# Grouped softmax, shared row memory and early loads in a two-layer graph attention kernel

## The chip, the cores and the metric

The kernel runs on one core of a Trainium2 chip. The core has TensorE (PE), VectorE (DVE), ScalarE (ACT), GpSimd (POOL) and SyncE (SP), and 16 DMA engines. The metric is the device time of one execution in microseconds; the figure shown for a kernel is the median of its runs.

## The reference

A graph of 10,000 nodes and 170,000 edges (80,000 random edges in both directions, and a loop at each node) goes through two graph attention layers, with residuals and layer norms. All of it is in float32; cut to what matters:

```python
def gat_conv(x, edge_index, W, a_src, a_dst, bias, heads, out_ch, concat):
    ...
    xl = (x @ W).reshape(n, heads, out_ch)
    alpha_src = jnp.einsum('nhc,hc->nh', xl, a_src)
    alpha_dst = jnp.einsum('nhc,hc->nh', xl, a_dst)
    e = jax.nn.leaky_relu(alpha_src[src] + alpha_dst[dst], 0.2)
    m = jax.ops.segment_max(e, dst, num_segments=n)
    e = jnp.exp(e - m[dst])
    s = jax.ops.segment_sum(e, dst, num_segments=n)
    alpha = e / (s[dst] + 1e-16)
    msg = xl[src] * alpha[:, :, None]
    out = jax.ops.segment_sum(msg, dst, num_segments=n)
    ...

h = gat_conv(x, edge_index, W1, a_src1, a_dst1, b1, 4, 256, True)
h = relu(layer_norm(h, g1, be1)) + (x @ Wr1 + br1)
h1 = h
h = gat_conv(h, edge_index, W2, a_src2, a_dst2, b2, 1, 768, False)
h = layer_norm(h, g2, be2) + (h1 @ Wr2 + br2)
return _layernorm(x + h)
```

`gat_conv` adds each node's loop a second time, so that a loop counts double (`doubled` in the kernel). Layer 1 has 4 heads of 256 columns (1024 in all), layer 2 one head of 768.

## The kernel before

**Stages.** First the kernel multiplies x by W1, node tile by node tile of 128 nodes (79 tiles), adds the two attention products of each node, and stores rows of 1033 numbers in a DRAM table (table1). Beside that it sorts the nodes by their number of edges and makes lists of neighbours. Then `ordered_layer1` and `ordered_layer2` each go through the 79 tiles. A tile holds 128 nodes with about equally many neighbours, and its work is done in "slots" or rows: row k holds, for each of the 128 nodes, the table row of its k-th neighbour. A tile has between 8 and 41 rows, 1377 in all. Layer 1's turns go up from 8 rows to 26, then take the tile of 41, then 27, 25, 24 and down to 9. Tiles of 22 rows and more are turns 34 to 45; turns 32, 33, 46 and 47 have 21 rows. Layer 2 goes from small to large tiles.

**The ring.** Rows are gathered from DRAM by GpSimd (L425, an indirect DMA for each row) into a ring of row places (`Ring`, 29 places of 1033 numbers in layer 1, 41 of 770 in layer 2). When row k of a tile is done with, `ring.fetch` asks for the row 29 (or 41) places further on. So a row's place must be free before its successor is asked for. After the logits of a set of rows, GpSimd also reads their last column (L490) and overwrites their attention columns (L491), in its own order between the gathers.

**A tile of layer 1.** `logits` (L479 to L487) adds the source and destination products of all of a tile's rows, applies the leaky relu, takes the maximum, subtracts it (VectorE) and takes the exponent (ScalarE). `normalised` (L498 to L504) divides by the sum. The weighted sum over the rows is then made by three engines. For the first `on_pe(t)` rows, at most 4, ScalarE makes diagonal matrices of the weights (L730) and TensorE multiplies them with the rows into a PSUM buffer acc (L736). Of the other rows VectorE does every fourth alone, with four multiply-adds of 256 columns (L521); for the rest ScalarE multiplies the row by its weights (L510) and VectorE adds it with one addition of 1024 columns (L517). ScalarE's multiplications are issued three rows ahead (`LEAD`). All of this is an order written out by hand, engine by engine (`manual_schedule`).

The generator `weights_of` does the logits and TensorE's share, and it is started for tile t+1 three rows before tile t ends, so that the next tile's logits stand in VectorE's order between the last rows of tile t. This is done only if the next tile's rows and 3 more fit in the ring (`SLOTS[t + 1] + LEAD <= ring.size`): not for the tiles of 27 and 41 rows. At the beginning of tile t come the layer norm of tile t-1 (`deviation`, `scaled`, L807), its transposition and the transposition of x (L708), the product with Wr1 (L172, 24 matmul records), and, two rows after TensorE's rows, `to_layer2` (L824 to L829): a store of the transposed h to h1_d and the product with W2 for layer 2's table, whose result is copied and stored by `store` in the next tile (L766, L768). `next_x` gathers the next tile's x and stores it to x_d (L697).

**The tile of 41 rows** doesn't fit the ring and goes through `attend_parts`: three parts, each with its own logits, a running maximum, sums on VectorE in a tile h of its own, and a rescaling of h when the maximum changes.

**Between the layers.** Layer 1's ring lies in a memory pool of that layer, layer 2's in one of its own, which may be used when layer 1's last store is through. Wr2 is loaded into Wr1's place by the first line of `ordered_layer2`. Then come, on SyncE's queue, h1 and x of the first two tiles (L911, L912) and five vectors spread over the partitions (L144), and on GpSimd's the gathers. br1 times Wr2 is made by TensorE: br1 is spread over 128 columns (brT, L905) and multiplied with Wr2 (`product`), then the residuals of tiles 0 and 1 (L988, L991), with tile 0's sums (L946) between them. The result of br1 times Wr2 is read after tile 0.

Of the kernel before, what the change touches and what calls it, by code (L numbers as in the profile page):

```python
# [35 lines left out]
P = 128  # L36
# [17 lines left out]
PARTED2 = 26  # L54

# [25 lines left out]
def gnn_kernel(ctx, tc, x, x_cols, src, dst, src_col, dst_col, W1, a_src1, a_dst1, b1, g1, be1, Wr1, br1,  # L81
# [359 lines left out]
    class Ring:  # L441
# [4 lines left out]
        def __init__(self, pool, table, row, size, own, at=None):  # L446
            self.table, self.size, self.own, self.issued = table, size, own, 0
            self.at = at or list(range(TOTAL))
            self.rows = pool.tile([P, size, row], F32, name="ring")
# [11 lines left out]

        def slot(self, q):
            return self.rows[:, q % self.size, :]

        def parts(self, lo, hi):

            while lo < hi:
                r = lo % self.size
                m = min(hi - lo, self.size - r)
                yield lo, lo + m, self.rows[:, r:r + m, :]  # L470
                lo += m
# [51 lines left out]

    def attend_parts(small, ring, acc, h_, ad, heads, dh, t, summed, between):


        c = heads * dh
        groups = -(-SLOTS[t] * 2 // ring.size)
        cuts = [FIRST[t] + SLOTS[t] * g // groups for g in range(groups + 1)]
        top = total = sums = None  # L530
        nc.vector.memset(acc[:, :c], 0.0)
        for lo, hi in zip(cuts, cuts[1:]):
            e, new = logits(small, ring, lo, hi, ad, heads, c, top)
            if lo == FIRST[t]:
                doubled(e, t)
            part = small.tile([P, heads], F32, name="part")
            nc.vector.reduce_sum(part, e.rearrange("p k h -> p h k"), axis=AX.X)
            if top is not None:
                nc.vector.tensor_add(acc[:, :c], acc[:, :c], sums[:, :c])
                fade = small.tile([P, heads], F32, name="fade")  # L540
                nc.vector.tensor_sub(fade, top, new)
                nc.scalar.activation(fade, fade, AF.Exp)
                for h in range(heads):
                    s = slice(h * dh, (h + 1) * dh)
                    nc.vector.tensor_scalar(acc[:, s], acc[:, s], fade[:, h:h + 1], None, op0=OP.mult)
                nc.vector.tensor_mul(fade, total, fade)
                nc.vector.tensor_add(part, part, fade)
            top, total = new, part
            m = min(ON_PE1, hi - lo - 1)
            pe = lo if hi == cuts[-1] else hi - m  # L550
            steps = summed(pe, e[:, pe - lo:], m)
            sums = next(steps)
            if pe == lo:
                for _ in steps:
                    pass
            alone = [q for q in range(lo, hi) if not pe <= q < pe + m]
            for k, q in enumerate(alone):
                shared = k >= len(alone) // 3
                if shared:
                    multiply(ring.slot(q), e[:, q - lo], dh)  # L560
                if k == len(alone) // 3 + 1:
                    for _ in steps:
                        pass
                weigh(acc, ring.slot(q), e[:, q - lo], dh, shared=shared)
                ring.fetch(q + 1 + ring.size)
            ring.fetch(hi + ring.size)
            between.pop(0)()
        nc.vector.tensor_add(acc[:, :c], acc[:, :c], sums[:, :c])
        divided(small, h_, acc, total, None, heads, dh)
# [111 lines left out]
    SLOTS1, FIRST1 = SLOTS, FIRST  # L681

# [3 lines left out]
    def ordered_layer1():  # L686
        nc.scalar.add_instruction(mybir.InstLoadActFuncSet(name=nc.get_next_instruction_name(), act_func_set_id=6, engine=nc.scalar.engine))
        with tc.tile_pool(name="b1", bufs=1) as pool, tc.tile_pool(name="small1", bufs=2) as small, \
                tc.tile_pool(name="ps_acc1", bufs=2, space=PSUM) as ps_acc, \
                tc.tile_pool(name="ps_h1", bufs=2, space=PSUM) as ps_half, \  # L690
                tc.tile_pool(name="ps_r1", bufs=1, space=PSUM) as ps_r, tc.manual_schedule():
            ring = Ring(pool, table1, R1, RING1, {})
# [25 lines left out]
            ring.fetch(RING1)  # L718
            g1_b, be1_b = (spread(pool, v, n) for v, n in ((g1, "g1"), (be1, "be1")))

            def on_pe(t):


                return min(max(SLOTS[t] // 2 - 5, 1), ON_PE1, SLOTS[t])

# [15 lines left out]
            def weights_of(t):  # L741

                n, m = SLOTS[t], on_pe(t)
                e, _ = logits(small, ring, FIRST[t], FIRST[t] + n, ring.slot(FIRST[t])[:, C1:C1 + H1], H1, C1)
                yield e
                normalised(small, e, H1, t)
                acc = ps_acc.tile([P, 2 * BANK], F32, name="acc")
                diagonals = pool.tile([P, ON_PE1 * H1, P], F32, name="diagonals")
                for lo, hi in ((0, min(m, 2)), (min(m, 2), m)):
                    summed(acc, diagonals, e, FIRST[t], lo, hi, m)  # L750
                    yield acc

            def shared(t, k):
                return (k - on_pe(t)) % SHARE > 0
# [16 lines left out]
            xT, moves = from_x(0)  # L771
            for move in moves:
                move()
            r = product(xT, wr1, C1, ps_r)
            for t in range(NT + 1):
# [3 lines left out]
                whole = live and n <= ring.size  # L779
                if whole and not ready:  # L780
                    ahead = weights_of(t)
                    ready += itertools.islice(ahead, 2)

                def multiplied(upto):
                    nonlocal done
                    while whole and done < min(upto, n):
                        if shared(t, done):
                            multiply(ring.slot(FIRST[t] + done), e[:, done], DH1)
                        done += 1

                if whole:
                    e, acc = ready
# [3 lines left out]
                for _ in ahead:  # L796
                    pass
# [6 lines left out]
                if last:  # L804
                    h = pool.tile([P, C1], F32, name="h")
                    scaled(h, [means[:, :C1]], stats, g1_b, be1_b)
                    nc.vector.scalar_tensor_tensor(h, h, 0.0, r_before[:, :C1], op0=OP.max, op1=OP.add)  # L807
                for move in moves:
                    move()
# [9 lines left out]
                if whole:  # L819
                    by_wr1()  # L820
# [12 lines left out]
                if last:  # L833
                    events.append((first + 2, to_layer2))
# [5 lines left out]
                if t + 1 < NT:  # L840
                    events.append((first + 2, next_x))

# [4 lines left out]
                if live and not whole:  # L847
                    due(first + 1)
                    sums, acc = (ps_acc.tile([P, 2 * BANK], F32, name="acc") for _ in range(2))
                    ad = small.tile([P, H1], F32, name="ad")  # L850
                    nc.vector.tensor_copy(ad, ring.slot(FIRST[t])[:, C1:C1 + H1])

                    def some(q, e, m):
                        diagonals = pool.tile([P, ON_PE1 * H1, P], F32, name="diagonals")
                        for lo, hi in ((0, min(m, 2)), (min(m, 2), m)):
                            summed(sums, diagonals, e, q, lo, hi, m)
                            yield sums

                    h = pool.tile([P, C1], F32, name="h")
                    attend_parts(small, ring, h, acc, ad, H1, DH1, t, some,  # L860
# [481 lines left out]
```

## Time and profile before

| what | us |
|---|---|
| median of the runs shown (3 runs) | 5579.29 |
| lowest and highest of these | 5576.32, 5603.79 |
| the profiled execution's own time | 5572.26 |
| its span, first to last instruction | 5570.4 |
| TensorE busy in the span | 4887.3 (88%) |
| VectorE busy | 4269.6 (77%) |
| GpSimd busy | 3301.6 (59%) |
| ScalarE busy | 2815.1 (51%) |
| bytes moved by DMA | 1591.39 MB |

All of the readings are of the one profiled execution. A busy engine is one whose instructions overlap the time; TensorE's matmuls are pipelined, so its busy share isn't a share of its peak. The granted clock is the share of full speed that the throttle gave TensorE. "Idle before" is the time in which an engine stood still before a group of instructions, with what ended it. Lines like L521 are lines of the kernel before; in the changed kernel the numbers are others. In lists of stretches, the first column is the stretch from and to, in us from the span's start.

### The profile page before, as it was taken

What the parts mean: (1) busy time and instruction counts of PE and PEld (TensorE: products, weight loads), DVE (VectorE), ACT (ScalarE), POOL (GpSimd) and SP (SyncE); (2) the same over time, 40 slices, a digit from 0 to 9 for tenths busy, and PEclk for the clock granted to TensorE, in tenths of its full rate; (3) what the DMA queues carried; (4) which work ended last, traced back from release to release, by engine and by line L of the source; (5) the groups of instructions that cost most, each with busy time, mean ns of one, the idle gap of its engine ahead of it and who ended that gap; (6) DMA issues with size and microseconds to landing.
All of it is one profiled execution on the core that took longest, in us unless ns stands there. A gap on an engine that the chain in (4) does not pass through costs nothing. (4 is left out here: it accounts for less than half of the span.)

```text
span 5570.4 us, 59760 instructions
## 1 busy us (share of the span) xinstructions
PE 4887.3 (88%) x15188; PEld 2896.9 (52%) x15191; DVE 4269.6 (77%) x7513; ACT 2815.1 (51%) x8193; POOL 3301.6 (59%) x3407
## 2 busy tenths in 40 slices
PE   9999996999999876689999999899988888887775
PEld 3444443555565544455555555565655555554544
DVE  5883344999999887789999995888876776766676
ACT  3443343777878776678877773333322222222222
POOL 2446455556666666566666653666665666666664
PEclk9999998999999987899999999999998888888887
DMA  4323536999999987899999986999888888888885
GB/s 156 123 94 89 91 97 234 323 345 354 364 366 371 350 325 255 314 342 369 370 367 361 339 310 230 334 336 329 323 322 287 307 298 301 295 291 294 293 293 183
DMA packets 474308, 1591.39 MB, mean 286 GB/s; under 512 B 118327, under 2 KB 122487, under 8 KB 473958
## 3 DMA queue, kind: packets, MB, share of 16 engines
q0 software_dynamic: 322384, 1286.62, 64.5%
q1 hardware_dynamic: 149520, 297.43, 15.8%
q10 hardware_dynamic: 2054, 3.42, 0.2%
q8 instruction: 128, 2.10, 0.1%
q14 instruction: 222, 1.82, 0.1%
HBM read 1431.80 MB, written 177.29 MB: 289 GB/s over the span
## 5 line engine op out<-in xcount | busy, mean ns | idle before, releaser
L425 POOL DMA_INDIRECT ring<-table,slots x2675 | 2664.3, 996 | 1631.5 <-issue 662.2
L521 DVE SCALAR_TENSOR_TENSOR acc<-ring,e,acc 128x512 f32<-128x512 f32 (+1 forms) x2530 | 1579.0, 624 | 149.4 <-PE acc L736 46.5
L510 ACT ACTIVATE ring<-ring,e 128x256 f32<-128x256 f32 x3284 | 1338.4, 508 | 2.3 <-issue 2.2
L517 DVE TENSOR_TENSOR acc<-acc,ring 128x1024 f32<-128x1024 f32 x801 | 986.5, 1232 | 70.5 <-DVE acc L517 1.4
L991 PE MATMUL big<-wr,w 128*128 128x512 f32 (+1 forms) x2464 | 872.0, 500 | 111.3 <-issue 109.8
L946 PE MATMUL big<-ring,diagonals 128*128 128x256 f32 x2754 | 758.5, 433 | 206.8 <-issue 168.0
L172 PE MATMUL big<-w,xT 128*128 128x512 f32 x1896 | 827.2, 598 | 23.3 <-DMA w<-in_W_dram 9.4
L172 PE MATMUL big<-wr,xT 128*128 128x512 f32 x1896 | 831.7, 595 | 0.2 <-issue 0.2
L829 PE MATMUL half<-w,hT 128*128 128x512 f32 (+1 forms) x2528 | 830.4, 486 | 0.0
L946 PEld LDWEIGHTS big<-ring,diagonals 128*128 128x128 f32 x2754 | 593.8, 219 | 371.5 <-issue 235.1
L991 PEld LDWEIGHTS big<-wr,w 128*128 128x128 f32 x2464 | 481.3, 196 | 471.4 <-issue 439.5
L945 ACT ACTIVATE diagonals<-ident,e 128x128 f32<-128x128 f32 x1377 | 423.5, 388 | 598.4 <-remote 180.3
L829 PEld LDWEIGHTS half<-w,hT 128*128 128x128 f32 x2528 | 477.8, 189 | 372.3 <-issue 334.4
L736 PE MATMUL acc<-ring,diagonals 128*128 128x256 f32 x1912 | 474.8, 406 | 201.9 <-ACT diagonals L730 198.0
L172 PEld LDWEIGHTS big<-w,xT 128*128 128x128 f32 x1896 | 362.7, 192 | 483.7 <-issue 464.9
L172 PEld LDWEIGHTS big<-wr,xT 128*128 128x128 f32 x1896 | 356.0, 191 | 419.4 <-issue 419.4
L736 PEld LDWEIGHTS acc<-ring,diagonals 128*128 128x128 f32 x1912 | 384.6, 204 | 285.0 <-ACT diagonals L730 219.0
L583 ACT ACTIVATE sd<-mv,eps 128x1 f32<-128x1 f32 x237 | 69.3, 293 | 696.9 <-DVE mv L581 444.4
L667 DVE TENSOR_TENSOR scr<-big,ad_b 128x1024 f32<-128x1024 f32 x79 | 96.7, 1224 | 378.4 <-ACT row L664 330.7
L730 ACT ACTIVATE diagonals<-ident,e 128x128 f32<-128x128 f32 x956 | 293.0, 388 | 173.3 <-DVE e L501 144.6
L672 POOL TENSOR_TENSOR row<-row,none 128x1024 f32<-128x1024 f32 x79 | 187.2, 2369 | 264.5 <-ACT row L664 261.5
L670 ACT ACTIVATE scr<-scr 128x256 f32<-128x256 f32 x632 | 253.5, 402 | 120.3 <-DVE scr L667 120.3
(185 smaller groups left out, 3445.0 us busy)
## 6 DMA issues: line engine op xcount, KB each, us to landing
ring<-table,slots POOLq DMA_INDIRECT x2675
table<-row SPq DMA_DIRECT2D x79, 516.0 KB
h_d<-hT SPq DMA_DIRECT2D x79, 512.0 KB
w<-h_d SPq DMA_DIRECT2D x77, 512.0 KB
table<-row SPq DMA_DIRECT2D x79, 385.0 KB
ring<-table SPq DMA_DIRECT2D x79, 385.0 KB
xT<-in_x_cols_dram SPq DMA_DIRECT2D x79, 384.0 KB
x_d<-xt SPq DMA_DIRECT2D x79, 384.0 KB
```

Source lines behind the costliest of these rows:

```text
L172: nc.tensor.matmul(p[:, c:e], aT[:, j, :], w[:, j, c:e], start=(j == 0), stop=(j == k - 1))
L425: nc.gpsimd.indirect_dma_start(out=to, out_offset=None, in_=table, in_offset=bass.IndirectOffsetOnAxis(ap=index, axis=0), **more)
L510: nc.scalar.activation(row[:, s], row[:, s], AF.Copy, scale=e[:, h:h + 1])
L517: nc.vector.tensor_add(acc[:, :c], acc[:, :c], row[:, :c])
L521: nc.vector.scalar_tensor_tensor(acc[:, s], row[:, s], e[:, h:h + 1], (acc if first is None else first)[:, s], op0=OP.mult, op1=OP.add)
L670: nc.scalar.activation(m[:, s], m[:, s], AF.Copy, accum_out=row[:, C1 + i * H1 + h:C1 + i * H1 + h + 1])
L730: nc.scalar.activation(diagonals[:, k * H1 + i, :], ident, AF.Copy, scale=e[:, k, i:i + 1])
L736: nc.tensor.matmul(acc[:, c:d], diagonals[:, k * H1 + i, :], ring.slot(q + k)[:, c:d], start=(k == 0 and c % BANK == 0), stop=(k == m - 1 ...
L829: nc.tensor.matmul(q, hT[:, j, :], w2[:, j, c:c + q.shape[1]], start=(j == 0), stop=(j == K1 - 1))
L945: nc.scalar.activation(diagonals[:, (k - lo) % G, :], ident, AF.Copy, scale=e[:, k - lo, :])
L946: nc.tensor.matmul(to, diagonals[:, (k - lo) % G, :], ring.slot(at + k)[:, ON_PE2:C2], start=False, stop=(k == n - 1), skip_group_check=True)
L991: nc.tensor.matmul(r[:, c:d], hT[:, j, :], wr2[:, j, c:d], start=False, stop=(j == K1 - 1 and d < C2), skip_group_check=True)
```

## The change

Layer 1's tiles of 22 rows and more are done in groups: two groups, with 8 rows in the later one, and three groups for the tile of 41 rows (17, 12 and 12). `attend_parts` is gone. The first group is done as a whole tile was, but not normalised; a later group has logits of its own against the running maximum, started 8 rows before its first row. The factor `fade` rescales what was summed before, and the division by the total is put into the last group's weights and `fade`. TensorE sums a later group's first rows (`later_on_pe`: 1 to 4) into the PSUM buffer that the next tile will use, ScalarE copies that sum into the place of the group's first row, and VectorE adds it with the rescaling in one multiply-add for each head. The next tile's first logits are always started before the tile ends. In these tiles `to_layer2` comes 6 rows before the first cut.

The memory of the rows is one tile, made outside of both layers; layer 2's ring takes 38 of its 41 places from it and 3 from a tile of its own. `begin_layer2` loads h1 and x of layer 2's first two tiles and Wr2 in layer 1's last pass, and VectorE multiplies Wr2 by br1 and adds its 8 parts; TensorE then sums this over the partitions with a matrix of ones. The residuals of tiles 0 and 1 are both made before tile 0's sums. At the start of layer 1 the rows of tile 0 are asked for first, then the two vectors, then x of tile 1 and the rest of the ring.

```diff
+PARTED = 22
...
-        def __init__(self, pool, table, row, size, own, at=None):
+        def __init__(self, table, size, own, views, at=None):
...
+        def place(self, q):
+            r = q % self.size
+            for v in self.views:
+                if r < v.shape[1]:
+                    return v, r
+                r -= v.shape[1]
...
-    def attend_parts(small, ring, acc, h_, ad, heads, dh, t, summed, between):
...
+    def begin_layer2(mem):
...
+        firsts = [(at_end(C1), at_end(D0)) for _ in range(min(2, NT))]
+        for t, (hT, xt) in enumerate(firsts):
+            nc.sync.dma_start(hT, h1_d[turns[t]])
+            nc.sync.dma_start(xt, x_d[turns[t]])
...
+        load(wr2, Wr2)
+        br, ones = at_end(C2), at_end(P)
+        yield
+        nc.vector.memset(ones, 1.0)
+        nc.vector.tensor_scalar(br, wr2[:, 0, :], br1_c[:, 0:1], None, op0=OP.mult)
+        for k in range(1, K1):
+            nc.vector.scalar_tensor_tensor(br, wr2[:, k, :], br1_c[:, k:k + 1], br, op0=OP.mult, op1=OP.add)
+        yield wr2, firsts, br, ones, rest
...
-            ring.fetch(RING1)
+            ring.fetch(SLOTS[0])
...
+            def later_on_pe(t):
+                return min(max((SLOTS[t] - 20) // 2, 1), ON_PE1)
...
             def weights_of(t):
...
+                for lo, hi in zip(cuts[1:], cuts[2:]):
+                    e, new = logits(small, ring, at + lo, at + hi, ad, H1, C1, top)
+                    fade = small.tile([P, H1], F32, name="fade")
+                    nc.vector.tensor_sub(fade, top, new)
+                    nc.scalar.activation(fade, fade, AF.Exp)
+                    yield
+                    part = small.tile([P, H1], F32, name="part")
+                    nc.vector.reduce_sum(part, e.rearrange("p k h -> p h k"), axis=AX.X)
+                    nc.vector.tensor_mul(total, total, fade)
+                    nc.vector.tensor_add(total, total, part)
+                    top = new
+                    if hi == n:
...
+                    sums, m = accs[(t + 1) % 2], later_on_pe(t)
+                    diagonals = pool.tile([P, ON_PE1 * H1, P], F32, name="diagonals")
+                    summed(sums, diagonals, e, at + lo, 0, m, m)
+                    yield lo, (e, fade)
+                    nc.scalar.copy(ring.slot(at + lo)[:, :C1], sums)
+                    yield
+            def cuts_of(t):
+                n = SLOTS[t]
+                groups = 1 if n < PARTED else -(-2 * n // ring.size)
+                size = 8 if groups == 2 else (n - 5) // groups
+                return [0] + [n - size * g for g in range(groups - 1, -1, -1)]
...
+            xt = fetch_x(1)
+            ring.fetch(RING1)
...
-                    events.append((first + 2, to_layer2))
+                    events.append((cuts[1] - 2 * LEAD if len(cuts) > 2 else first + 2, to_layer2))
...
-                if whole and t + 1 < NT and SLOTS[t + 1] + LEAD <= ring.size:
+                if live and t + 1 < NT:
                     ahead = weights_of(t + 1)
-                for k in range(n if whole else 0):
+                for k in range(n):
+                    if k + 2 * LEAD + 2 in cuts[1:-1]:
+                        next(later)
+                    if k + 2 * LEAD in cuts[1:-1]:
+                        lo, es_lo = next(later)
+                        es[lo] = es_lo
...
+                    if k + 2 in cuts[1:-1]:
+                        next(later)
+                    weights, fade = row_of(k)
+                    if fade is not None:
+                        for h in range(H1):
+                            s = slice(h * DH1, (h + 1) * DH1)
+                            nc.vector.scalar_tensor_tensor(acc[:, s], acc[:, s], fade[:, h:h + 1], ring.slot(FIRST[t] + k)[:, s],
+                                                           op0=OP.mult, op1=OP.add)
...
-            q = product(brT, wr2, C2)
-            rs = {0: residual(0)}
+            q = ps_big.tile([P, 2 * BANK], F32, name="big")
+            for c in range(0, C2, BANK):
+                d = min(C2, c + BANK)
+                nc.tensor.matmul(q[:, c:d], sums_of, br[:, c:d], start=True, stop=True)
+            rs = {t: residual(t) for t in range(2)}
...
+        with tc.tile_pool(name="rows", bufs=1) as rows_pool:
+            mem = rows_pool.tile([P, RING1 * R1], F32, name="ring")
+            ordered_layer2(mem, ordered_layer1(mem))
```

## The prediction

> **What bounds the kernel now.** I read the page first, then busy times in stretches cut at each node tile's store of h1_d, then the waits of VectorE in the stretch that stands out, then the timeline between the two layers.
>
> ```profile
> PE 4887.3 (88%) x15188; PEld 2896.9 (52%) x15191; DVE 4269.6 (77%) x7513; ACT 2815.1 (51%) x8193; POOL 3301.6 (59%) x3407
> ```
>
> No engine is the bound throughout, so the span has to be cut. Layer 1 runs from about 885 to 3409 us, layer 2 to 5558. The stretches of layer 1 (columns: length, then busy time of PE, PEld, DVE, ACT, POOL, granted clock, DMA share, GB/s):
>
> ```profile
> 2565.23:2597.61 32.38, 29.85 (x104) 17.96 (x103) 29.68 (x44) 27.16 (x74) 22.23 (x24) 1.00 0.99 367
> 2386.81:2424.16 37.35, 32.02 (x104) 19.80 (x103) 33.09 (x50) 28.88 (x78) 24.24 (x28) 0.91 0.93 337
> 2301.34:2345.41 44.07, 32.24 (x104) 19.90 (x103) 35.58 (x52) 32.83 (x86) 25.47 (x30) 0.85 0.90 329
> 2113.66:2206.11 92.45, 58.72 (x207) 40.78 (x208) 64.70 (x123) 60.05 (x171) 61.83 (x62) 0.80 0.60 204
> 2206.11:2256.38 50.27, 32.50 (x104) 20.16 (x103) 40.12 (x58) 35.26 (x94) 28.71 (x33) 0.80 0.85 309
> 1835.97:2532.82 696.85, 524.80 (x1698) 327.00 (x1697) 573.91 (x862) 501.48 (x1341) 427.87 (x464) 0.86 0.87 317
> ```
>
> These are, in order, tiles of 20, 22, 24, 41 and 27 table rows, and all sixteen tiles of 21 rows and more (two of them 21 at each end). At 20 rows VectorE is idle 2.70 us of 32.38: it is the bound, and the 2.70 us are the small gaps between its some 45 instructions. At 24 rows it is idle 8.5 us, at 27 rows 10.2, at 41 rows 27.8. In the whole stretch it idles 696.85 - 573.91 = 122.9 us, of which 16 x 2.70 = 43 are ordinary. The other 80 are what a change can take. What it waits for there:
>
> ```profile
> DVE e L479 <- DMA ring<-table,slots: 39.0, 10, 7.7
> DVE acc L521 <- PE acc L736: 23.3, 15, 4.3
> DVE h L517 <- ACT ring L510: 6.9, 15, 1.7
> DVE e L479 <- issue: 3.0, 2, 2.5
> DVE e L479 <- POOL ring L491: 2.6, 1, 2.6
> DVE h L531 <- PE half L708: 2.3, 1, 2.3
> DVE e L479 <- POOL slots L490: 2.0, 1, 2.0
> ```
>
> L479 starts a tile's logits, which need all of its rows, three rows before the tile ahead ends. The ring has 29 rows, so the last row of a tile of n takes a place freed only 27 - n rows of work before: three at 24, and it hasn't landed. The L479 lines sum to 46.6 us. The two lines of tile h, with some small ones, are the 41-row tile's own path.
>
> **Part 1, softmax in groups** (11 tiles of 22 to 27 rows in two groups, the 41-row tile in three: 13 later groups). The first group has 14 to 19 rows, so its last place came free 13 to 8 rows of work before; a row is on average (2.06 + 3 x 1.30) / 4 = 1.49 us (timeline: four 256-wide multiply-adds 2.06, three wide adds 3.91), so that is at least 11.9 us. The later group's logits come eight rows before its first row, for rows asked for long before. The L479 waits should go: 46.6 us. attend_parts goes, with its waits (6.9 + 2.3 and 1.8 of smaller ones) and most of the 4.3 us for PE at its start: 15.3. Gone: 62 us.
>
> What it adds, on VectorE, the bound. The built programs' counts: 256-wide multiply-adds and scalings 1280 -> 1300, 1024-wide adds 824 -> 808, and some 130 small ones (logits again, fade, total). The rows:
>
> ```profile
> L517 DVE TENSOR_TENSOR acc<-acc,ring 128x1024 f32<-128x1024 f32 x801 | 986.5, 1232 | 70.5 <-DVE acc L517 1.4 <-remote 1.2 <-issue 0.9
> L521 DVE SCALAR_TENSOR_TENSOR acc<-ring,e,acc 128x256 f32<-128x256 f32 x1232 | 603.2, 490 | 105.4 <-PE acc L736 46.5 <-remote 18.7 <-issue 0.4
> ```
>
> +20 x 0.49 = +9.8; -16 x 1.23 = -19.7; small ones take 0.17 to 0.29 us (the group lines of the softmax), 0.22 with their gap, so +130 x 0.22 = +28.6. Net +18.7 us. Two ways to close the sum: waits less additions, 62 - 18.7 = 43; or new busy time plus ordinary idleness, 573.9 + 18.7 + 43.2 = 636, a gain of 61. They differ by waits for PE's sums. I take 48, nearer the first, since PE gets more work: 72 more 256-wide sums at 0.47 us (eight records of L736, two to a sum, take 1.89 us) are 34 us, and its waits won't shrink. Per tile that is 1.9 us (22 rows) to 5.6 (26 and 27), in about 7 us of PE idleness; unhidden it would be the whole 34. ScalarE gains a 1.0 us copy, a small exp and 4 diagonals per row given to PE for each group, some 3 us where it is idle over 8.
>
> New waits. ScalarE's copy of the sums into the group's first row waits for PE; behind it on ScalarE stand the multiplied rows, and VectorE's first row of the group waits for it. At 22 rows PE has the 10.5 us product with Wr1 and then 1.9 us of sums, starting 2.0 us after VectorE's first row (as the timeline of the 20-row tile has it): 14.4, copied at 15.4. VectorE gets there after 3 rows at 2.06 and 7 at 1.30 plus 2.6 us of small work, at 17.9. Slack 2.5 us, gone when the granted clock falls to 0.83. The product with w2, with its h1_d store, moves from two rows after the PE rows to 6 before the cut, behind the sums: PE ends it by about 30 us of 39, and its reader, the next tile's store, comes after. On SP the h1_d store now stands behind x_d's, which waits some 9 us for its gather (2424.2 to 2433.6); its source hT is overwritten a tile later, and the row store behind it comes 30 us later. The other PSUM buffer is free once the tile before is scaled, at the tile's start.
>
> The clock: in the stretches above 2.5 us of PE idleness (20 rows) go with 1.00, 5.3 (22 rows) with 0.91, 11.8 (24 rows) with 0.85. The tiles in groups keep about 7 us, so I expect some 0.9 there; PE's 31.8 us at 22 rows become 35, still under VectorE's 38.9, and this too is why I stay near 43. [...]
>
> **Part 2, between the layers.**
>
> ```profile
> 3413.41 12.28 PE L172 MATMUL big<-wr,ring 128*128 128x512 f32 x32 [4.42 <-DVE ring L905]
> 3425.53 1.02 PE L988 MATMUL big<-ring,ident 128*128 128x512 f32 x2
> 3435.43 0.17 DVE L479 TENSOR_TENSOR e<-ring,ad 128x8 f32<-128x8 f32 x1 [7.26 <-DMA ring<-table,slots]
> 3449.45 0.17 DVE L479 TENSOR_TENSOR e<-ring,ad 128x10 f32<-128x10 f32 x1 [3.01 <-DMA ring<-table,slots]
> ```
>
> PE loses the 12.28 us of br1 times Wr2 for two matmuls of about 1.6 (the L988 rows, 1.02 at 512 wide and 0.59 at 256), and starts at 3409.4, when ScalarE's last copy begins to free its buffers, rather than 3413.4: 14.7 us. But table rows land no sooner: the gathers still wait for the last table2 store, and from 3413 the DMA engines are full. What helps there is that two h1 and x pairs and one direct row, 2 x 0.92 + 0.39 = 2.2 MB, move into an empty stretch after 3380: at the some 390 GB/s of the stretches from 3440 to 3480 5.7 us. On SP they stand ahead of the Wr2 load, which waits for PE until 3387 anyway; behind them come a row store at 3397.7 and h1_d at 3399, not delayed. VectorE's 8 passes over Wr2 (1.02 us each, by the 128x768 row of L595) fit into its idleness from 3392 to 3412, as Wr2 lands near 3397; uncovered they cost 8. residual(1) ahead of tile 0's sums ends at 3434, when those start. From tile 2 on PE leads again, so 5.7 to 13; I take 7.
>
> **Part 3, small things.** Layer 1's start: the second x gather passes 21 ring gathers on POOL and waits for x_d's store; POOL, free at 924 now, ends near 930; tile 1's rows, needed at 933.9, come first. Nothing, -3 to +3; without that cover, 6. The ring in two memories splits some of layer 2's logits: 25 ops x 0.2 = 5 us of an engine with slack; I take 2.
>
> Sum: 48 + 7 - 2 = 53 us off the profiled 5572.3 (span 5570.4 and 1.9 around it). The median shown is 5579.3, 7 us above that execution; taking the same off it gives **5526**.
>
> **Rivals.**
> 1. All waits go and PE's lead at the layers' border holds: 61 + 13 = 74 and nothing lost elsewhere, 5505. For it: at 20 rows nothing but 2.70 us is idle. Against: PE's clock.
> 2. Half of the L479 waits stay (23 us), moved to the first group or to full queues, and 10 us of PE's 34 show: 48 - 33 + 7 = 22, 5557. For it: DMA shares of 0.97 to 1.00 at 18 to 20 rows. Against: the stretch moves 317 GB/s, those rows 367 and more.
> 3. Slower: the copy of the sums comes late. If the 10.5 us product with w2 got ahead of the sums on PE, each of 13 later groups would wait 10.5 - 2.5 = 8 us: 104, 5630. It decides from 4.1 us late per group, where the 53 us of gain are gone. Against: the sums are issued first.
> 4. That the change doesn't do what it says: the groups are in the counts, so no chance apart.
>
> **How the numbers follow.** Forecast 0.66 (5510 to 5550), rival 1 0.11, rival 2 0.13, rival 3 0.10. A measurement tells 0.5%, 28 us, from no change: faster is below 5551, the forecast and rival 1, 0.77; same 0.13; slower 0.10. The range 5497 to 5563 takes in the most of rivals 1 and 2 and leaves out rival 3.
>
> **What would show it.** The sixteen tiles near 649 us; the first-logits line with under 10 us of waits on DMA; the 41-row tile near 65; tile 0 of layer 2 starting its logits 16 us, not 22, after the first gather. Wrong if VectorE's fade rows wait on ScalarE's copy, or the first-logits waits stay above 20 us.

## The result, and the profile after

| | before | after |
|---|---|---|
| median, us (4 runs each) | 5577.81 | 5542.27 |
| lowest and highest | 5573.78, 5603.79 | 5538.32, 5546.93 |
| profiled execution: span | 5570.4 | 5542.8 |

The ratio of the times is 0.9931, with a 95% interval of 0.9906 to 0.9956: 35.5 us by the medians, 27.6 by the spans of the two profiled executions. The forecast was 53 us and 5526; the time lies within the range given, at about two thirds of the gain.

Lines of the kernel after: logits L489 (before L479), wide addition L527 (L517), multiply-add L531 (L521), TensorE's sums L731 (L736), the row with the fade L917 (new), ScalarE's copy of the sums L778 (new), layer 2's sums L988 (L946), residuals L1030 and L1033 (L988, L991), br1 times Wr2 summed over partitions L1059 (in place of L172).

Stretches of layer 1 after, cut as before at the stores of h1_d (length, then busy time of PE, PEld, DVE, ACT, POOL, granted clock, DMA share, GB/s): the same turns in the same order, 20, 22, 24, 41 and 27 rows, then all sixteen.

```profile
2527.71:2561.07 33.36, 29.85 (x104) 17.97 (x103) 29.78 (x44) 27.16 (x74) 22.20 (x24) 1.00 0.98 355
2354.61:2394.07 39.46, 34.83 (x119) 21.99 (x118) 36.19 (x65) 30.98 (x85) 26.13 (x31) 0.96 0.95 334
2274.21:2313.73 39.52, 34.87 (x115) 22.21 (x114) 34.63 (x61) 34.17 (x93) 25.26 (x31) 0.91 0.96 344
2118.34:2187.70 69.36, 46.94 (x160) 29.02 (x158) 55.17 (x96) 54.28 (x146) 46.98 (x54) 0.88 0.88 307
2187.70:2231.03 43.33, 36.73 (x126) 23.70 (x126) 37.85 (x72) 35.19 (x96) 28.52 (x34) 0.96 0.96 356
1838.81:2495.31 656.50, 555.97 (x1842) 348.77 (x1841) 579.65 (x988) 516.03 (x1396) 423.25 (x486) 0.94 0.94 336
```

Within tiles in groups the store of h1_d comes later than it did, so single stretches are cut elsewhere than before; the sixteen together begin and end in tiles that are not in groups, and there the comparison is clean: 696.85 to 656.50, 40.35 us. VectorE's idle time fell from 122.9 to 76.9 us, its work rose from 573.91 to 579.65. What VectorE waits for in the sixteen tiles after (us in total, times, longest):

```profile
DVE acc L531 <- PE acc L731: 15.8, 14, 2.2
DVE acc L527 <- remote: 5.5, 1, 5.5
DVE e L489 <- DMA ring<-table,slots: 4.2, 5, 1.7
DVE acc L531 <- PE half L697: 4.1, 2, 2.2
DVE acc L527 <- ACT ring L520: 1.9, 1, 1.9
...
DVE acc L917 <- ACT ring L778: 0.2, 1, 0.2
```

The first-logits line on DMA was 39.0 us and is 4.2. The row with the fade waits once, for 0.2 us. VectorE's waits for TensorE ahead of its multiply-adds hardly changed: 19.9 us (15.8 and 4.1) after 23.3.

Between the layers, on TensorE (start, us, engine, line, operation, and in brackets the idle time before with what ended it):

```profile
3374.19 1.53 PE L1059 MATMUL big<-ring 128*128 128x512 f32 x4 [0.51 <-issue]
...
3398.87 0.69 PE L992 MATMUL big<-b,ones 1*128 1x256 f32 x2
3400.90 3.72 PE L988 MATMUL big<-ring,diagonals 128*128 128x256 f32 x16 [1.33 <-DMA ring<-table,slots]
```

The product of 12.28 us has become one of 1.53 us, both residuals are done by 3398.9, and TensorE then has to wait for the rows, 1.33 us here.

### The profile page after: what moved, and what is told of

Read it like the earlier page. It is cut to its first block, busy times and chain, and to the rows that moved or that the text cites. A ratio compares the mean times of both kernels' runs of the same rounds, so it can differ in the third digit from the quotient of the medians.

```text
span 5542.8 us, 60338 instructions
## 1 busy us (share of the span) xinstructions
PE 4908.0 (89%) x15304; PEld 2913.5 (53%) x15307; DVE 4286.7 (77%) x7678; ACT 2828.9 (51%) x8248; POOL 3296.8 (59%) x3429
## 5 line engine op out<-in xcount | busy, mean ns | idle before, releaser
L531 DVE SCALAR_TENSOR_TENSOR acc<-ring,e,acc 128x256 f32<-128x256 f32 (+1 forms) x2546 | 1586.7, 623 | 141.6 <-PE acc L731 44.0
L520 ACT ACTIVATE ring<-ring,e 128x256 f32<-128x256 f32 x3232 | 1320.8, 508 | 1.4 <-issue 1.3
L527 DVE TENSOR_TENSOR acc<-acc,ring 128x1024 f32<-128x1024 f32 x808 | 995.1, 1232 | 78.1 <-remote 5.5
L1033 PE MATMUL big<-wr,w 128*128 128x512 f32 (+1 forms) x2464 | 875.8, 501 | 142.1 <-issue 138.2
L988 PE MATMUL big<-ring,diagonals 128*128 128x256 f32 x2754 | 750.4, 431 | 197.5 <-issue 149.1
L988 PEld LDWEIGHTS big<-ring,diagonals 128*128 128x128 f32 x2754 | 590.4, 218 | 360.9 <-issue 226.9
L1033 PEld LDWEIGHTS big<-wr,w 128*128 128x128 f32 x2464 | 482.2, 196 | 503.6 <-issue 471.9
L987 ACT ACTIVATE diagonals<-ident,e 128x128 f32<-128x128 f32 x1377 | 423.1, 388 | 609.8 <-remote 228.6
L731 PE MATMUL acc<-ring,diagonals 128*128 128x256 f32 x2056 | 514.3, 406 | 138.2 <-ACT diagonals L725 99.5
L731 PEld LDWEIGHTS acc<-ring,diagonals 128*128 128x128 f32 x2056 | 411.0, 203 | 237.8 <-ACT diagonals L725 125.2
L725 ACT ACTIVATE diagonals<-ident,e 128x128 f32<-128x128 f32 x1028 | 315.4, 388 | 173.2 <-DVE e L511 115.8
```

Source lines behind the costliest of these rows:

```text
L520: nc.scalar.activation(row[:, s], row[:, s], AF.Copy, scale=e[:, h:h + 1])
L527: nc.vector.tensor_add(acc[:, :c], acc[:, :c], row[:, :c])
L531: nc.vector.scalar_tensor_tensor(acc[:, s], row[:, s], e[:, h:h + 1], (acc if first is None else first)[:, s], op0=OP.mult, op1=OP.add)
L725: nc.scalar.activation(diagonals[:, k * H1 + i, :], ident, AF.Copy, scale=e[:, k, i:i + 1])
L731: nc.tensor.matmul(acc[:, c:d], diagonals[:, k * H1 + i, :], ring.slot(q + k)[:, c:d], start=(k == 0 and c % BANK == 0), stop=(k == m - 1 ...
L987: nc.scalar.activation(diagonals[:, (k - lo) % G, :], ident, AF.Copy, scale=e[:, k - lo, :])
```

## The experiments

Each kernel is the changed one with one edit. Ratios are to the kernel before on the same chip. The runs fell on several chips, whose times for the same kernel differ (medians of the kernel before from 5232.15 to 5586.24 us); so layer 1's sixteen tiles are read beside the ratio. The kernel before was profiled once, beside the result: a stretch of a later run set against it can differ by the chip too.

**1. The changed kernel again, twice**, on two chips.

> The changed kernel once more, to see how far two profiled executions of the same layer 2 differ. Theory 1 (the 7 us lost between layer 2's tiles 3 and 60 are a difference of executions): layer 2 from its fourth output to its last differs by 2 us and more from the first profile's. Rival B (they belong to the program): it agrees within 1 us. Layer 1's sixteen tiles within 2 us of 656.5 either way.

> The changed kernel beside the other two on one chip. Theory 1 (the change earns about 40 us of layer 1, and what layer 2 does varies by chip and execution): layer 1 from its first store of h1_d to its last 2404 to 2414 us, eighteen tiles 718 to 723, whatever layer 2 lasts; ratio to before 0.992 to 0.994.

Ratios 0.9926 (0.9908 to 0.9945) and 0.9939 (0.9925 to 0.9954). Sixteen tiles 654.8 and 653.3 us. Layer 1 from its first store of h1_d to its last took 2413, 2408 and 2406 us in the three profiles, against 2450 before. Layer 2 from its fourth output to its last took 2029.6, 2021.7 and 2024.2, with 2021.2 before: the some 8 us by which the first profile was longer than before shrink to 0.5 and 3.0. Theory 1 holds in that they are no fixed part of the program; whether they go with the execution or with the chip isn't separated, since the two repeats ran on different chips.

**2. The groups alone**: layer 2 and its beginning as before.

```diff
-            ordered_layer2(mem, ordered_layer1(mem))
+            ordered_layer1(mem)
+        ordered_layer2()
...
+            load(wr2, Wr2)
+            mem = pool.tile([P, RING2 * R2], F32, name="ring")
...
+            q = product(brT, wr2, C2)
+            rs = {0: residual(0)}
```

> Layer 1 as changed, layer 2 and its beginning as before (own ring in one piece, late loads, br1 times Wr2 on TensorE). Theory 1 (nearly all of the gain is the grouped softmax; what the layers' border wins is spent again within layer 2's first three tiles): median within 4 us of the changed kernel's 5542, the sixteen tiles 655 to 658 us long, layer 2's first output 4 us later than in the changed kernel and its third not later at all. Rival A (the border is worth the 7 us forecast): median near 5549. Rival B (the ring in two pieces costs layer 2 the some 7 us by which its lead shrank between tile 3 and the end): median near 5535 to 5538, and layer 2 from its fourth output to its last is 7 us shorter than in the changed kernel.

**3. The border alone undone**, the shared memory and the ring in two pieces kept.

```diff
+            load(wr2, Wr2)
+            rest = mem.shape[1]
...
+            q = product(brT, wr2, C2)
+            rs = {0: residual(0)}
```

> Grouped softmax and shared row memory with layer 2's ring in two pieces, but the loads of layer 2 late, br1 times Wr2 on TensorE and tile 1's residual in its old place. Theory 1: within 4 us of the changed kernel and of the kernel with groups alone. Rival A (border worth 7 us): 7 us over the changed kernel, near 5549. Rival B (two pieces cost 7 us): layer 2 from its fourth output to its last as long as in the changed kernel, and 7 us longer than with groups alone.

Medians on one chip: groups alone 5521.2, border undone 5516.7, the changed kernel 5518.3; ratios 0.9927 (0.9904 to 0.9949), 0.9930 (0.9908 to 0.9952) and 0.9926. All of the measurable gain is there with the groups alone (which keep layer 1's new start too); the border is worth less than these intervals can show. Layer 2's first outputs, in us after the last store of h1_d:

| kernel | 1st | 2nd | 3rd | 4th | 5th |
|---|---|---|---|---|---|
| before | 91.1 | 103.7 | 122.1 | 138.2 | 153.4 |
| groups alone | 91.3 | 104.5 | 121.7 | 138.0 | 152.3 |
| border undone | 86.2 | 106.4 | 126.1 | 143.7 | 160.1 |
| changed, three profiles | 86.8, 86.4, 85.2 | 103.1, 102.6, 102.1 | 120.0, 118.8, 119.6 | 137.8, 136.0, 137.0 | 154.2, 152.4, 153.4 |

The changed kernel is 4 to 6 us ahead at the first output and level at the fifth. The two pieces' cost isn't seen either: on this one chip the rest of layer 2 lasted 2015.5 us with one piece, 2021.7 (changed) and 2005.8 (border undone) with two; rival B had both of the latter 7 us over the former, and the last is 9.7 below it. Over all chips but the fastest it lasted 2005.8 to 2041.1 us in eight profiles with two pieces, 2021.2 and 2015.5 in the two with one. Why the kernel with the border undone is 5 us late at its fourth output stays open; it was made up again later.

What happens to the border's lead shows in the 100 us that follow the last store of h1_d, before and after (columns as in the stretches above):

```profile
3399.04:3499.04 100.00, 88.24 (x287) 53.72 (x285) 46.30 (x110) 18.24 (x58) 56.72 (x60) 0.97 0.89 326
```

```profile
3363.72:3463.72 100.00, 70.77 (x216) 43.12 (x215) 50.05 (x111) 18.25 (x58) 58.66 (x60) 0.85 0.84 300
```

TensorE works 17.5 us less, of which 10.8 are the removed product (12.28 less 1.53); it idles instead, and the granted clock falls from 0.97 to 0.85. The DMA engines move 30.0 MB instead of 32.6, and GpSimd issues as many operations (60) in both: the 2.2 MB that were moved ahead leave the DMA engines idle here (a share of 0.84 where 0.89 was), and no further rows come in their place.

**4. Only the tiles of 27 and 41 rows in groups.**

```diff
-PARTED = 22
+PARTED = 27
```

> Only the tiles of 27 and 41 rows are done in groups; those of 22 to 26 rows are whole again, ten tiles. Theory 1 (the first-logits waits of all these tiles were what the groups took away; the 41-row tile and its neighbour won 16 and 7 us, the other ten some 17): the sixteen tiles near 674 us, the first-logits line on DMA back to some 15 to 25 us of waits, the median near 5560. Rival C (the ten tiles only trade waits for the added logits, fade and sums; all of the gain is the 41-row path and the 27-row tile): the sixteen tiles near 657 and the median within 4 us of 5542. Rival D (whole tiles of 24 to 26 rows suffer more once the 41-row path is gone): above 680.

Ratio 0.9957 (0.9939 to 0.9975), sixteen tiles 672.63 us. The first-logits wait is back with 34.9 us, more than the 15 to 25 that theory 1 gave, and all but 0.2 us of it stand before whole tiles (waits of VectorE there):

```profile
DVE e L489 <- DMA ring<-table,slots: 34.9, 12, 6.6
```

So the ten tiles earned 17.8 us (672.63 against 654.82, same chip), for 32.0 us of these waits less (34.9 against 2.9). The rest went into 9.6 us of added work (579.76 against 570.18 busy) and some new small waits. The 41-row tile and its neighbour earned about 24.2 (696.85 - 672.63, against the one profile before). Theory 1, which expected 674, holds; rival C's 657 and rival D's 680 and more fall.

**5. The third rival made real**: the product with w2 ahead of the later group's sums.

```diff
-                    events.append((cuts[1] - 2 * LEAD if len(cuts) > 2 else first + 2, to_layer2))
+                    events.append((first + 2, to_layer2))
```

> The product with w2 (10.5 us on TensorE) two rows after TensorE's rows in the tiles in groups too, so ahead of the later group's sums, instead of 6 rows before the first cut. This is the third rival's mechanism made real. Theory 1 (ScalarE's copy of the sums ends on average some 1.9 us ahead of VectorE's row with the fade, 0.0 to 3.2 in 13 groups): at 22 rows that row is late by 10.5 - 1.9 = 8.6 us, less in larger tiles, where the cut lies up to 5 rows, 7.5 us, later: 12 tiles by about 5, 60 us, the sixteen tiles near 715, waits of the fade row on ScalarE's copy 40 to 80 us; the rival's flat 8 us for 13 groups, 104, is the upper end (760). Rival E (what VectorE waits there it gets back at the tile's end, since TensorE has its work done earlier and VectorE's waits for the first sums, 16 us, go): the sixteen tiles below 680.

Ratio 1.0049 (1.0032 to 1.0065), slower than the kernel before, on a chip where the changed kernel itself didn't run; sixteen tiles 731.73 us. VectorE's waits there:

```profile
DVE acc L917 <- ACT ring L778: 81.8, 12, 8.2
DVE acc L531 <- PE acc L731: 21.1, 16, 2.4
```

The row with the fade waits, 6.8 us on average in twelve groups, and is the new first line; theory 1 had 40 to 80 us for it. The length lies between theory 1's 715 and the 760 of the rival's flat price. Rival E, below 680, falls, and the waits for the first sums, which it took away, are still 21.1. In the changed kernel that line has 0.2 us, since the sums stand first:

```profile
1921.25 1.23 DVE L527 TENSOR_TENSOR acc<-acc,ring 128x1024 f32<-128x1024 f32 x1
1922.59 2.08 DVE L917 SCALAR_TENSOR_TENSOR acc<-acc,fade,ring 128x256 f32<-128x256 f32 x4
```

This is VectorE in a 22-row tile. ScalarE's copy ran from 1919.75 to 1920.76, 1.83 us ahead of L917. Over the 13 groups that slack was 0.03 to 3.2 us.

**6. One row, or four, of each later group on TensorE** (the change gives it 1 to 4).

```diff
-                return min(max((SLOTS[t] - 20) // 2, 1), ON_PE1)
+                return 1
```

> TensorE sums 1 row of each later group instead of 1 to 4; 13 rows go from TensorE to VectorE and ScalarE. Theory 1 (VectorE is the bound of these tiles, TensorE's 34 us of added sums are hidden): VectorE gains 13 rows at 1.49 us, 19 us, all of it on the path: sixteen tiles near 674. Rival G (TensorE's added sums cost as well, through VectorE's waits for them, 16 to 20 us): the waits for sums shrink below 10 us and the sixteen tiles stay within 5 us of 655.

```diff
+                return ON_PE1
```

> TensorE sums 4 rows of every later group; 26 more rows go from VectorE to TensorE. VectorE loses 26 at 1.49 us, 39 us; TensorE gains 26 at 1.89 us, 49 us, and comes to some 605 busy of 655. Theory 1 (VectorE the bound, but TensorE next within reach): the copy of the sums comes 5.7 us later at 22 rows, 3.8 behind VectorE's fade row, so part of it comes back as waits on that copy (30 us or more) and the sixteen tiles land between 640 and 665. Rival H (VectorE is the bound and TensorE has room): near 620. Rival G (TensorE is already the bound): above 675.

Both ran on one chip, that of experiment 5, and are compared with each other first: ratios 0.9920 (0.9904 to 0.9937) and 0.9862 (0.9846 to 0.9879), and the sixteen tiles with one row and with four (columns as in the stretches above):

```profile
1821.19:2485.41 664.22, 538.26 (x1738) 335.03 (x1737) 598.43 (x1013) 514.19 (x1380) 419.87 (x486) 0.90 0.92 332
```

```profile
1826.51:2457.82 631.31, 577.76 (x2050) 376.20 (x2049) 542.31 (x941) 515.21 (x1424) 423.07 (x486) 0.97 0.95 349
```

From one to the other 39 rows go from VectorE to TensorE; VectorE's busy time falls from 598.43 to 542.31, 1.44 us a row, and 32.9 of these 56.1 us reach the end. VectorE sets the pace there, though not alone. The waits for sums were 18.2 and 13.1 us, so giving TensorE fewer rows doesn't lower them, and rival G, which had them below 10, falls. One row came 10 us below theory 1's 674: of the 19 us of work that it adds only part arrives, some 8 to 13 over the 651.7 to 656.5 of the changed layer 1 on other chips. Four rows landed below what theory 1 gave, 640 to 665, and above rival H's 620. The waits on the copy, which theory 1 put at 30 us or more, were 6.7; the longest line of VectorE's waits there is for ScalarE's multiplied rows:

```profile
DVE acc L527 <- ACT ring L520: 26.5, 23, 2.5
```

**7. Four rows again, on another chip.**

> The kernel with 4 rows on TensorE in every later group once more. On a chip where layer 2 takes 1700 us from its fourth output to its last it had eighteen tiles in 698.0 us and a ratio to before of 0.9862; with the 21-row tiles in groups as well, on a chip where layer 2 takes 2020 us, 719.9. Theory 1 (it is the program: four 21-row tiles in groups with 4 rows on TensorE cost the 22 us): 695 to 703 on any chip, ratio to before near 0.988 where layer 2 takes 2020 us. Rival J (it is the chip: where instructions reach the engines with gaps, ScalarE's added diagonals come late): 708 to 722 on a chip where layer 2 takes 2020 us, ratio near 0.992. If it falls on a chip with 1700 us again, that stays open.

Ratio 0.9943 (0.9923 to 0.9963), sixteen tiles 652.92 us, eighteen tiles 719.4: rival J's 708 to 722 holds, and theory 1's 703 falls; the ratio came a little above the 0.992 that J had. The same kernel is 21.6 us shorter on the one chip; VectorE is equally busy on both, 542.3 and 542.6. On the second, VectorE waits longer for ScalarE's multiplied rows:

```profile
DVE acc L527 <- ACT ring L520: 33.4, 12, 7.0
```

ScalarE is equally busy too (515.2 and 517.6 us), but on the second chip it stands 20.1 us in gaps that end with nothing the profile shows, 7.8 of them ahead of its multiplications and diagonals, where its list of waits on the first has none. TensorE has 20.7 us of the like, but 16.5 of these are one gap that ends 0.45 us after ScalarE began the tile's diagonals. So gaps of ScalarE's own are there; what part of the 21.6 us they make, and what the added diagonals make, stays open.

**8. The tiles of 21 rows in groups too**, with the change's rows on TensorE, with n - 19 and with 4.

```diff
-PARTED = 22
+PARTED = 21
...
-                return min(max((SLOTS[t] - 20) // 2, 1), ON_PE1)
+                return min(max(SLOTS[t] - 19, 1), ON_PE1)
```

> The four tiles of 21 rows are done in groups as well. Theory 1 (groups pay where whole tiles wait for their last rows): the 21-row tiles last 34.7 to 37.4 us, some 2 to 5 over the 32.4 of the 20-row tiles, of which 1.5 are the row more; grouping removes at most 1 to 3 us each and adds 1.3: sixteen tiles within 4 us of 655, no difference in the median. Rival F (their waits are as large as at 22 rows and go too): sixteen tiles 8 us shorter, near 647.

> Tiles of 21 rows in groups too, and TensorE sums n - 19 rows of a later group, 1 to 4, instead of (n - 20) / 2: 2 at 21 rows, 3 at 22, 4 from 23 on. The four tiles of 21 rows shift the markers at both ends of the sixteen tiles, so eighteen tiles are read, from the store two turns before to the one after (722.9 us in the changed kernel, 698.0 with 4 rows everywhere, 717.5 with the 21-row tiles in groups). Theory 1 (VectorE's work is the bound until TensorE's 37 us a tile are reached): 698 less 4 for the tiles of 21 rows and 4 to 8 for their second row and TensorE's freed place at 22: 686 to 692. Rival I (TensorE is the bound once it has 4 rows, and 21-row tiles only exchange one for the other): 695 to 700.

> The same with 4 rows on TensorE in every later group, the tiles of 21 rows too. Theory 1: at 21 rows TensorE comes to 30 us and four rows at 1.89, 37.6, more than such a tile lasts now (34.7 to 36.5): eighteen tiles 4 to 8 us longer than with n - 19 rows. Rival H (TensorE has room): 4 to 8 us shorter.

Since 21-row tiles mark both ends of the sixteen, eighteen tiles are read (761.8 before, 722.9, 721.6 and 721.7 in the changed kernel). With the change's rows 717.5 us, ratio 0.9893 (0.9877 to 0.9910), on the chip of experiment 6, where the changed kernel itself didn't run; its first figure, sixteen tiles in 645.08, agrees with rival F's 647 only because the markers moved. With n - 19 rows 716.7, ratio 0.9918 (0.9905 to 0.9931); with four 719.9, 0.9926 (0.9914 to 0.9938); the changed kernel beside these two has 0.9939 (0.9925 to 0.9954). The forecasts of 686 to 700 for n - 19 rows were built on the 698.0 of the one chip and missed. Four rows were 3.2 us longer than n - 19, the way theory 1 had it and short of its 4 to 8. A gain of 2 to 5 us in layer 1 over the changed kernel on the same chip (721.7) is all that these show, and in the whole time the intervals overlap: no version is shown to beat the changed kernel on every chip.

## Why the prediction was right or wrong

**The mechanism was right.** The waits of a tile's first logits for its last rows were the loss, and grouping removes them: 46.6 us of idle time ahead of these instructions before, 6.1 after, and back by experiment 4 where the tiles are whole again. The copy of the sums is in time, with 1.83 us to spare at 22 rows where 2.5 was forecast. Undoing the order that keeps it in time costs 6.8 us on average in twelve groups, where the third rival had 8 in thirteen; that rival's place and condition were right.

**Part 1 was mis-sized: 48, measured 40.35** (42 to 45 in four further profiles with the same layer 1, against the one profile before). Of its two ways the first, waits less additions, gave 43 and was the better one; the 48, chosen part of the way to 61, was the step that failed. Inside the 43 two errors cancel. The waits gone were put at 62: VectorE's idle time fell by 46.1. Some 6 us of first-logits waits stay, and 9.2 us of waits stand at the row additions, where 1.9 were (6.9 more were `attend_parts`' own); 5.5 of them are a single one in the 41-row tile, whose stretch is 69.4 us where 65 was forecast (in the first repeat the like is 5.2 us, and the profile puts it down to ScalarE's multiplied rows). The added work was put at 18.7: VectorE's busy time rose by 5.7. The 256-wide and 1024-wide operations came out nearly as counted (+20 and -16, +11.4 and -19.7 us where +9.8 and -19.7 were forecast); the small ones, 123 more, take 19.4 us together, 0.16 each and partly under their neighbours, where 0.22 with a gap was taken.

**TensorE's added sums**: 34 us forecast, 31.2 measured (524.80 to 555.97), and its idle time in these tiles fell from 172 to 101 us while VectorE waited no longer for it: they were hidden. Experiment 6 shows the same from the other side, where the tiles grew as TensorE's sums were taken away. TensorE's 35 us at 22 rows came out (34.83 in the stretch above); the 38.9 us for VectorE beside it follow from no row that the forecast shows, and that stretch has 36.19 us of VectorE in 39.46.

**The clock** went from 0.86 to 0.94 in the sixteen tiles ("some 0.9" was said). In the 26 us from 3397.72, where TensorE works 13.1 and waits for rows, the granted clock is 0.80, and from 3443.72 to 3473.72, with 20.4 of 30 busy, 0.72 (0.78 in the like place before, from 3479.04 to 3509.04, with 16.4 of 30 busy). So a low clock goes with idle time in both places, though not in proportion: at the layers' border, in the 100 us of experiment 3, TensorE's idle time rises from 11.8 to 29.2 us with the change and the clock falls from 0.97 to 0.85; in the sixteen tiles its idle time falls from 172 to 101 us and the clock rises. The record of the clock in the two traces, before and after, holds only the values 1.0 and 0.5; in the sixteen tiles TensorE had 0.5 for 191 us before and 85 after. What the higher clock itself was worth wasn't separated.

**Part 2 was wrong in size: 7 forecast; measured 0.4 to 2.2 us at layer 2's fourth output, -0.8 to 1.0 at the fifth.** Tile 0's logits start 20.1 us after the first gather, not 16 (22.2 before). The step that failed is "From tile 2 on PE leads again, so 5.7 to 13". The rows of the third tile did land 3.7 us sooner (its logits 60.3 us after the last store of h1_d, 64.0 before), but TensorE spent its lead waiting (13.1 of the 26 us from 3397.72 busy), and the lead was gone by the fifth output. What takes it from the rows wasn't isolated. A patch in which TensorE passes one matmul in 2.1 to 3.5 us, shown at the end, lies there in both kernels (from 3492 to 3510 us before, 3438 to 3456 after).

**Part 3**: layer 1's start, forecast 0 (-3 to +3), came out between -1.8 and +2.8 us at the first store of h1_d (948.9 before, 947.1 to 951.7 in nine profiles on chips like the first). The ring in two pieces, forecast -2, can't be told from nothing. What was not in the sum are 1 to 2 us that layer 1 loses after the sixteen tiles (866.2 us before, 867.1 to 868.4 in five profiles of the changed layer 1).

So the sum read 53 = 48 + 7 - 2. The runs say 40 to 45 in the sixteen tiles, less 1 to 2 behind them, and nothing measurable from the border on; by the three ratios 34 to 41 us arrive at the end.

**The two nearer rivals.** Rival 1, 74 us, needed all waits gone and the lead kept, and neither came. Rival 2 had 22 us, and the 34 to 41 lie between it and the forecast; but its cause didn't occur: 6.1 of the 46.6 us of first-logits waits stay, not half, and the waits for TensorE's sums didn't grow by 10.

## What to carry to other kernels

A wait at the start of a tile for data whose place the tile before still holds was cured here by starting on the part that has long been there (46.6 us of idle time became 6.1); count it as the waits named in the trace less the added work, which gave 43 where 40.35 were measured, and expect some new waits where the old ones ended, here 9.2 us at the row additions in place of 1.9. A lead given to an engine that next waits for a transfer can be lost again: here the third tile's rows landed 3.7 us sooner, the first output came 4 to 6 us ahead, and by the fifth nothing was left. Where an engine gets a short new task that another waits for, its place in the queue can matter more than its length: here the place was worth 81.8 us of waits (experiment 5), and two rows more on average in thirteen groups 6.7 (experiment 6).

## What the runs showed of the hardware

One chip ran layer 2 far faster than the others with the same program: the kernel before has a median of 5232 us there and of 5557 to 5586 in the other sets of runs. The kernel of experiment 6 with four rows, from layer 2's fourth output to its last, on that chip (columns as in the stretches above; then TensorE's longest waits there):

```profile
3452.10:5149.81 1697.71, 1542.60 (x5413) 1056.87 (x5411) 1510.95 (x3036) 560.54 (x1770) 1247.62 (x1293) 0.94 0.96 357
```

```profile
PE big L988 <- ACT diagonals L987: 102.9, 27, 14.2
PE big L992 <- ACT big L1018: 30.7, 3, 16.2
PE big L988 <- DMA ring<-table,slots: 10.7, 6, 3.5
```

The same kernel on another chip:

```profile
3496.11:5518.72 2022.61, 1674.45 (x5451) 1106.87 (x5449) 1515.52 (x3036) 569.82 (x1771) 1254.66 (x1293) 0.89 0.86 300
```

```profile
PE big L988 <- issue: 156.4, 98, 8.9
PE big L1033 <- issue: 125.2, 108, 3.2
```

On the second, TensorE stands 281.6 us in waits that end with nothing the profile shows, up to 2.5 us each mostly, nearly all before matmuls of 256 columns; on the first its list of waits, shown whole above, has none. Of the 325 us by which the stretch is longer there, TensorE idles 193 and is busy 132 more, at a granted clock of 0.89 in place of 0.94. The kernel before and the changed kernel have the like on such chips, 268 to 272 us in the same two lines. They are the largest item of TensorE's waits in layer 2 there, and neither kernel touches them. They are thickest in the patch at the layers' border, 15.8 of the 20 us from 3438, on TensorE in the changed kernel:

```profile
3438.74 0.38 PE L988 MATMUL big<-ring,diagonals 128*128 128x256 f32 x1 [2.20 <-issue]
3441.54 0.59 PE L988 MATMUL big<-ring,diagonals 128*128 128x256 f32 x1 [2.42 <-issue]
```

One matmul of 0.4 to 0.6 us passes in 2.8 (once in 2.1), seven times on end, when the DMA engines have just run at a share of 1.00 for 46 us. The profile lists two instruction queues: in the two stretches above they moved the same 50 and 72 packets on both chips (131 and 225 in the whole executions), and between 3438 and 3457 us, while seven gaps passed, none. What makes the gaps, no run here shows.
